# Depthwise convolution taken chunk by chunk, with the next image's normalised input written into freed chunks and an image's gates issued among the next image's taps

## The chip, the cores and the metric

The kernel runs on one NeuronCore of a Trainium2 chip. The metric is the time of one execution on the device, in microseconds; lower is better. Five engines work side by side, each through its own list of instructions, in order: TensorE (PE in the profile, with its weight loads as PEld), VectorE (DVE), ScalarE (ACT), GpSimd (POOL) and SyncE (SP, which here only issues DMAs). An instruction that waits holds up everything behind it in its engine's list.

## What is computed

Two layers over `x` of shape (4, 384, 32, 32): four images, 384 channels, 1024 positions each. All is float32.

```python
x = x + attention(ln_c(x))                 # 8 heads, relative position tables
t = tokens(x); t = t + gelu(ln_t(t) @ w_fc.T) @ w_proj.T      # w_fc, w_proj are Kronecker products
x = image(t)
# layer 1
out = dw(x, w77) + dw(x, w53) + dw(x, w35) + dw(dw(x, w7w), w7h) + dw(dw(x, w5w), w5h) + bias
x = x + out                                # where x inside dw(...) is ln_c(x)
t = tokens(x); u = ln_t(t)
masked = top-2 of softmax(u @ gate_w + gate_b), renormalised      # 4 experts
t = t + sum over e of masked[e] * (gelu(u @ w1[e] + b1[e]) @ w2[e] + b2[e])
```

The five depthwise convolutions are folded into one 7x7 kernel per channel: 49 taps.

## The kernel before

Three phases follow each other. `qkv_phase` writes queries, keys and values to DRAM. `attention_phase` goes through the eight heads and writes `ao_d`; its order is pinned by hand. `rest_phase`, the only one that the change touches, does everything behind the attention. A scheduler lays out its instructions for each engine: what is written earlier in the program comes first, and what is ready may be drawn forward where an engine would otherwise idle by the scheduler's own reckoning. The order on each engine is then fixed.

An image `b` goes through these steps in `rest_phase`. The 384 channels lie as three chunks `k` of 128 partitions, in the tile `xb` (two buffers, so two images at a time).

- `front(b)`: for each half of 512 positions, load `at` (attention output) and the half of `x`, project (L750), add (L753), then the Kronecker feed-forward (L775 to L785).
- `image(xb)`: for each half, statistics over channels (L71 to L79), spread over the partitions (L88, L90), subtract the mean into `xc` (L799, VectorE), multiply by the scale into the padded `img` (L802, GpSimd, all three chunks in one instruction).
- `convolve(b, xb)`: add the bias to `xb` (L813, three instructions), then 49 steps of three taps. A tap is one VectorE instruction, `xb[k] += img[k, shifted] * w7[k]` (L818, 128x1024). The three chunks take turns, so a tap's accumulator was last written three taps earlier. At the end `xb` is stored to `x2_d` (L823).
- `gates(g, b, xb)`: normalise the tokens (L71 to L79, L852), gate scores on TensorE (L537), softmax and top 2 on VectorE (L543 to L571, some forty small instructions that depend on each other).
- `scatter(g)`: after the last image of a group, `slot_positions` computes for each token its slot in a buffer sorted by expert (L617 to L682; L682 writes the weight rows `row`, L663 the slots `pos`), and GpSimd scatters the token rows into `xs_d` by indirect DMA (L862, 16 DMAs per image).

The groups are `((0,), (1,), (2, 3))`. `blocks(g)` runs the experts' feed-forward on blocks of 128 slots: 19 blocks for each of the first two groups, 35 for the third, 73 in all. A block loads its rows (`xg`, L882), transposes them (L888), copies them to `xT` (L889, VectorE), does 36 matmuls `e_ps` (L921) with 12 Gelu instructions (L924) and 12 matmuls `y_ps` (L904), and ends in `yo` (L907, VectorE). The weights of half a block come by an indirect DMA on GpSimd (L894). `combine(g)` gathers two rows per token and adds them to `x2_d`.

The order around the change: image 0 goes through all its steps before any block; `front(1)` runs among the taps of image 0. The steps of images 1 to 3 (`rest_of`) are handed out by `more()`, which `blocks` calls 12 times a block, at a fixed rate over the 38 blocks of the first two groups: 216 steps in 456 calls, one step being three taps. A group's blocks are written only after its own scatter.

Of the kernel before, what the change touches and what calls it, by code (L numbers as in the profile page):

```python
# [10 lines left out]
F32 = mybir.dt.float32  # L11
AF = mybir.ActivationFunctionType
# [5 lines left out]
P = 128  # L18
# [36 lines left out]
def bcast(ap, dim, n):  # L55

    dims = [list(d) for d in ap.ap]
    dims[dim] = [0, n]
    return bass.AP(ap.tensor, ap.offset, dims)


def token_stats(nc, pools, ident, x, eps, rows=None):


    small, psum, tag = pools
    nj = TOK // P
    mv = small.tile([P, nj, 2], F32, tag="s_mv", name="s_mv")
    for j in range(nj):
        ps = psum.tile([P, TOK], F32, tag=tag, name="row_ps")
        for k in range(KC):  # L70
            nc.tensor.transpose(ps[:, k * P : (k + 1) * P], x[:, k, j * P : (j + 1) * P], ident)  # L71
        st = small.tile([P, 6], F32, tag="s_st", name="s_st")
        nc.vector.bn_stats(st, ps[:, :C])  # L73
        nc.vector.bn_aggr(mv[:, j, :], st)
        if rows is not None:
            nc.scalar.copy(rows[j], ps[:, :C])
    rstd = small.tile([P, nj, 1], F32, tag="s_rstd", name="s_rstd")
    nc.scalar.activation(rstd, mv[:, :, 1:2], AF.Sqrt, bias=eps)
    nc.vector.reciprocal(rstd, rstd)  # L79
    return mv[:, :, 0:1], rstd  # L80


def to_partitions(nc, pools, ident, one, values):

    small, psum, tag = pools
    nj = values.shape[1]
    dg = small.tile([P, nj, P], F32, tag="s_dg", name="s_dg")
    nc.vector.tensor_tensor(dg, bcast(ident.unsqueeze(1), 1, nj), bcast(values, 2, P), ALU.mult)  # L88
    ps = psum.tile([P, TOK], F32, tag=tag, name="all_ps")
    nc.tensor.matmul(ps, one, dg.rearrange("p j n -> p (j n)"), start=True, stop=True)  # L90
    return ps
# [593 lines left out]
def rest_phase(tc, cst, x, ao_d, ins, slots, x2_d, out):  # L685
# [9 lines left out]
    with ExitStack() as es:  # L695
# [41 lines left out]
        def front(b, xb):  # L737

            for half in range(2):
                n0 = half * TOK  # L740
                xs = xb[:, :, n0 : n0 + TOK]
                at = ld.tile([P, KC, TOK], F32, tag="at", name="at", bufs=1)
                nc.sync.dma_start(
                    at, ao_d[:, b * N + n0 : b * N + n0 + TOK].rearrange("(k p) n -> p k n", p=P)
                )
# [41 lines left out]
                    )  # L787
                    yield

        def image(xb):  # L790

            rows = IMG // 2
            for half in range(2):
                xs = xb[:, :, half * TOK : (half + 1) * TOK]
                mean, rstd = token_stats(nc, stp, ident, xs, cst["eps6"])
                mps = to_partitions(nc, (small, ps_m, "m"), ident, one, mean)
                sps = to_partitions(nc, (small, ps_m, "m"), ident, one, rstd)
                xc = work.tile([P, KC, TOK], F32, tag="xc", name="xc", bufs=1)
                nc.vector.tensor_tensor(xc, xs, bcast(mps.unsqueeze(1), 1, KC), ALU.subtract)  # L799
                scale_sb = work.tile([P, TOK], F32, tag="scale", name="scale")  # L800
                nc.scalar.copy(scale_sb, sps)
                nc.gpsimd.tensor_tensor(  # L802
                    img[:, :, 3 + half * rows : 3 + (half + 1) * rows, 3 : 3 + IMG],
                    xc.rearrange("p k (y x) -> p k y x", x=IMG),
                    bcast(scale_sb.rearrange("p (y x) -> p y x", x=IMG).unsqueeze(1), 1, KC),
                    ALU.mult,
                )
                yield

        def convolve(b, xb):  # L810

            for k in range(KC):
                nc.vector.tensor_scalar_add(xb[:, k, :], xb[:, k, :], cbias[:, k : k + 1])  # L813
            acc = xb.rearrange("p k (y x) -> p k y x", x=IMG)
            for dy in range(7):
                for dx in range(7):
                    for k in range(KC):
                        nc.vector.scalar_tensor_tensor(  # L818
                            acc[:, k], img[:, k, dy : dy + IMG, dx : dx + IMG], w7[:, k, dy, dx : dx + 1],
                            acc[:, k], ALU.mult, ALU.add,  # L820
                        )
                    yield
            nc.sync.dma_start(x2_d[:, b * N : (b + 1) * N].rearrange("(k p) n -> p k n", p=P), xb)  # L823

        groups = []
# [145 lines left out]
            xbs[b] = xp_.tile([P, KC, N], F32, tag="xb", name="xb")  # L971
            yield from front(b, xbs[b])

        def rest_of(b):

            yield from image(xbs[b])
            ahead = enter(b + 1) if b + 1 < B else iter(())
            for _ in convolve(b, xbs[b]):
                next(ahead, None)
                yield  # L980
            yield from ahead
            yield from gates(owner[b], b, xbs[b])
            if b == owner[b]["images"][-1]:
                yield from scatter(owner[b])
            yield "end"

        def steps_of(images):
            for b in images:
                yield from rest_of(b)

        for _ in enter(0):
            pass
        for _ in rest_of(0):
            pass
        todo = steps_of(range(1, B))
        total = 3 * 62 + 30
        done = [0, 0.0]
        rate = total / (NF * sum(g["nb"] for g in groups[:-1]))
        behind = iter(())
# [113 lines left out]
```

## Time and profile before

| | |
|---|---|
| three timed runs | 3903.89, 3910.33, 3932.67 us (median 3910.33) |
| the profiled execution, its own time | 3887.36 us |
| its span in the profile | 3885.6 us |
| PE busy | 3212.3 us (83%) |
| DVE busy | 2335.8 us (60%) |
| ACT busy | 1250.2 us (32%) |
| POOL busy | 1129.4 us (29%) |
| `rest_phase` (from its first projection to the end) | 1898 to 3886 us |
| taps of image 0 | 2019.05 to 2209.4 us |
| `yo` of block 1, 38, 39 | 2327.33, 3230.36, 3258.34 us |

All durations below come from the profiled execution. Busy time is the union of an engine's instructions; instructions of one engine overlap by a little, so the time from start to start is shorter than the mean duration of one. The number behind `x` is a count.

### The profile page before, as it was taken

The numbers are of one execution on the slowest core, as the hardware profiler recorded it, in microseconds if no ns is written. First come the engines' busy times: TensorE is split into PE (matmuls) and PEld (weight loads), VectorE is DVE, ScalarE is ACT, GpSimd is POOL, SyncE is SP. The second block draws the span as 40 slices with busy tenths as digits, with TensorE's granted clock in tenths as the row PEclk, the third lists the DMA queues.
The fourth block names the chain that finished last, engine by engine and source line by source line (L and its number), as shares of the span: only waits on it lengthen the run. The fifth ranks groups of instructions, "written<-read, shape, count | busy, mean of one in ns | idle before, by whom it ended". The sixth has DMA issues, their size and how long they took to land.

```text
span 3885.6 us, 63554 instructions
## 1 busy us (share of the span) xinstructions
PE 3212.3 (83%) x25493; PEld 2161.8 (56%) x25493; DVE 2335.8 (60%) x3495; ACT 1250.2 (32%) x2502; POOL 1129.4 (29%) x1043
## 2 busy tenths in 40 slices
PE   8977878878787888878665549999998899999993
PEld 4535555555555555545321235574576677777772
DVE  2237777777787877868359958858889921000002
ACT  0124444444444444535111112242232132222220
POOL 3116253535344443526000031131132142111113
PEclk9989999999999998989887569999999899999996
DMA  7344444435363535253200141252143445223304
GB/s 274 127 151 113 132 120 111 139 92 166 71 181 74 181 74 173 72 163 85 76 16 8 37 159 57 106 220 72 66 153 148 152 156 191 79 77 131 130 21 130
DMA packets 195110, 455.06 MB, mean 117 GB/s; under 512 B 67008, under 2 KB 131536, under 8 KB 186880
## 3 DMA queue, kind: packets, MB, share of 16 engines
q1 hardware_dynamic: 145792, 216.99, 18.0%
q0 software_dynamic: 38400, 183.39, 12.8%
q10 hardware_dynamic: 10624, 50.62, 6.1%
q8 instruction: 201, 3.29, 0.4%
q14 instruction: 93, 0.76, 0.1%
HBM read 557.33 MB, written 144.31 MB: 181 GB/s over the span
## 4 chain that ended last, share of the span: by engine, by line
PE 33%; DVE 13%; DMA 3%; issue 2%; POOL 1%; ACT 1%; SPq 0%; POOLq 0%; DVEq 0%; ACTq 0%
PE e_ps L921 13%; PE y_ps L904 12%; DVE xb L818 10%; PE f_ps L775 2%; PE o_ps L778 2%; PE proj_ps L750 1%; DMA yt<-y_d,pos 1%; PE gate_ps L537 1%; PE row_ps L71 1%; DMA w<-in_w,row 1%; PE xT_ps L888 0%; DMA xg<-xs_d 0%; PE ffn_ps L784 0%; DVE xb L813 0%; DVE s_st L73 0%
## 5 line engine op out<-in xcount | busy, mean ns | idle before, releaser
L311 POOL TENSOR_TENSOR bias<-b,s 128x416 f32<-128x416 f32 (+24 forms) x656 | 660.9, 1042 | 829.6 <-DMA qs<-qk_d 502.6
L921 PEld LDWEIGHTS e_ps<-xT,w 128*128 128x128 f32 x5256 | 721.0, 196 | 297.1 <-issue 90.5
L921 PE MATMUL e_ps<-xT,w 128*128 128x128 f32 x5256 | 751.8, 282 | 33.6 <-DVE xT L889 25.1
L904 PE MATMUL y_ps<-w,eh 128*128 128x384 f32 x1752 | 711.4, 492 | 8.6 <-ACT eh L924 8.6
L818 DVE SCALAR_TENSOR_TENSOR xb<-img,w,xb 128x1024 f32<-128x1024 f32 x588 | 712.2, 1274 | 0.0
L924 ACT ACTIVATE eh<-e_ps,w 128x128 f32<-128x128 f32 x876 | 320.0, 367 | 1002.6 <-PE e_ps L921 1001.9
L894 POOL DMA_INDIRECT w<-in_w,row x146 | 214.3, 1468 | 1316.3 <-DVE yo L907 372.9
L354 ACT ACTIVATE arow<-arow,nm 128x1024 f32<-128x1024 f32 x256 | 295.9, 1156 | 297.2 <-DVE nm L344 297.1
L375 ACT COPY aT<-t_ps 128x512 f32<-128x512 f32 x512 | 275.7, 588 | 310.0 <-PE t_ps L374 301.5
L374 PEld LDWEIGHTS t_ps<-ident,arow 128*128 128x128 f32 x2048 | 228.5, 145 | 255.0 <-ACT arow L354 191.9
L202 PE MATMUL sc_ps<-kq,qs 48*32 48x512 f32 x2048 | 291.3, 632 | 88.6 <-DVE nm L344 59.4
L365 DVE TENSOR_REDUCE extra<-arow 128x32 f32<-128x32 f32 (+24 forms) x512 | 356.4, 737 | 0.0
L374 PE MATMUL t_ps<-ident,arow 128*128 128x128 f32 x2048 | 289.8, 286 | 71.1 <-ACT arow L354 56.4
L344 DVE CUSTOM_DVE_ANT_0 arow<-sc_ps,bias 128x1024 f32<-128x1024 f32 x256 | 310.7, 1214 | 36.5 <-POOL bias L311 36.2
L274 DVE STREAM_TRANSPOSE b<-tabk_ps 128x960 f32<-128x960 f32 x128 | 229.3, 1826 | 134.9 <-PE tabk_ps L202 119.8
L202 PE MATMUL tabk_ps<-tab,kq 48*128 48x480 f32 x512 | 261.3, 650 | 37.0 <-DMA kq<-qk_d 29.8
L202 PE MATMUL sc_ps<-k,kq 48*32 48x512 f32 x2048 | 291.3, 632 | 0.0
L904 PEld LDWEIGHTS y_ps<-w,eh 128*128 128x128 f32 x1752 | 272.0, 194 | 22.5 <-ACT eh L924 11.0
L202 PE MATMUL tabq_ps<-tab,kq 48*128 48x480 f32 x512 | 252.9, 639 | 37.0 <-DMA kq<-qk_d 28.3
L907 DVE TENSOR_TENSOR yo<-y_ps,w 128x384 f32<-128x384 f32 x73 | 40.5, 555 | 395.8 <-PE y_ps L904 395.6
L202 PEld LDWEIGHTS av_ps<-aT,vb 128*64 128x64 f32 x4096 | 227.5, 139 | 51.4 <-ACT aT L375 26.0
L202 PE MATMUL av_ps<-aT,vb 128*64 128x128 f32 x4096 | 242.9, 278 | 0.0
(158 smaller groups left out, 3542.2 us busy)
## 6 DMA issues: line engine op xcount, KB each, us to landing
sd<-st SPq DMA_DIRECT2D x128, 480.0 KB, 2.5
s<-sd SPq DMA_DIRECT2D x512, 120.0 KB, 3.0
tvw<-in_tv ACTq DMA_DIRECT2D x120, 192.0 KB, 3.6
xg<-xs_d SPq DMA_DIRECT2D x73, 192.0 KB, 2.4
y_d<-yo SPq DMA_DIRECT2D x73, 192.0 KB, 1.9
qk_d<-qk_sb POOLq DMA_DIRECT2D x48, 256.0 KB, 2.3
kq<-qk_d ACTq DMA_DIRECT2D x16, 768.0 KB, 12.0
v_d<-va POOLq DMA_DIRECT2D x4, 2048.0 KB, 8.0
```

The costliest lines, as they stand in the source:

```text
L202: pin(nc.tensor.matmul(*args, **kw))
L274: nc.vector.transpose(b2.rearrange("p e y x -> p x (e y)")[:, i : i + 2], ps[:, :, : SPAN * IMG])
L311: nc.gpsimd.tensor_tensor(bias[:, y0:y1, :], bass.AP(b2.tensor, b2.offset + (e * IMG + y0) * IMG, [list(b2.ap[0]), [(step * IMG + 1) * IMG ...
L344: nc.vector.tensor_tensor_reduce(s["flat"], ps.rearrange("p h n -> p (h n)"), s["bias"].rearrange("p y x -> p (y x)"), -SCALE, BIG, ALU.ad ...
L354: nc.scalar.activation(s["flat"], s["flat"], AF.Exp, bias=s["nm"], scale=-1.0, accum_out=dn[:, y % YT : y % YT + 1])
L365: pin(nc.vector.tensor_reduce(ex[:, i, :], a[:, p0:p1, :].rearrange("p y x -> p x y"), AX.X, ALU.add))
L374: pin(nc.tensor.transpose(pt[:, j, :], s["flat"][:, k0 : k0 + P], ident))
L375: pin(nc.scalar.copy(aT[:, 4 * g : 4 * g + 4, s["y"] % YB, :], pt))
L818: nc.vector.scalar_tensor_tensor(acc[:, k], img[:, k, dy : dy + IMG, dx : dx + IMG], w7[:, k, dy, dx : dx + 1], acc[:, k], ALU.mult, ALU.add,)
L904: nc.tensor.matmul(py, hs, w[:, o : o + C], start=(ff == 0), stop=(ff == NF - 1))
L921: nc.tensor.matmul(ph, w[:, o : o + P], xT[k][:, c, :], start=(c == 0), stop=(c == KC - 1))
L924: nc.scalar.activation(hs, ph, AF.Gelu, bias=w[:, o : o + 1])
```

## The change

The convolution loop is turned round: the chunk is the outer loop, the 49 taps the inner one, so consecutive taps write the same accumulator. `image` is split. `image_parts(b)` makes `xc` and the scale and adds the bias, now on ScalarE; `image(b, k)` multiplies one chunk into `img` (L812, two instructions of a third of the size), and is called for the next image as soon as the chunk's 49 taps of this image are written and `image_parts` is through. `convolve` now carries a generator `beside(b)`: the gates and scatter of the image before, then `front` and `image_parts` of the next image, one step of it beside two of every three taps. `xc` has two buffers instead of one, and `at` shares them. A step of `todo` is now one tap: 471 steps for the same 456 calls. Image 0's gates and scatter still come before any block.

```diff
-                at = ld.tile([P, KC, TOK], F32, tag="at", name="at", bufs=1)
+                at = work.tile([P, KC, TOK], F32, tag="xc", name="at")
...
+        def image_parts(b):
             for half in range(2):
-                xs = xb[:, :, half * TOK : (half + 1) * TOK]
+                xs = xbs[b][:, :, half * TOK : (half + 1) * TOK]
                 mean, rstd = token_stats(nc, stp, ident, xs, cst["eps6"])
+                yield
...
-                xc = work.tile([P, KC, TOK], F32, tag="xc", name="xc", bufs=1)
+                xc = work.tile([P, KC, TOK], F32, tag="xc", name="xc")
...
+                parts[b].append((xc, scale_sb))
+                yield
+            for k in range(KC):
+                nc.scalar.activation(xbs[b][:, k, :], xbs[b][:, k, :], AF.Identity, bias=cbias[:, k : k + 1])
+            yield
+
+        def image(b, k):
+            rows = IMG // 2
+            for half, (xc, scale_sb) in enumerate(parts[b]):
                 nc.gpsimd.tensor_tensor(
-                    img[:, :, 3 + half * rows : 3 + (half + 1) * rows, 3 : 3 + IMG],
-                    xc.rearrange("p k (y x) -> p k y x", x=IMG),
+                    img[:, k, 3 + half * rows : 3 + (half + 1) * rows, 3 : 3 + IMG],
+                    xc[:, k, :].rearrange("p (y x) -> p y x", x=IMG),
...
-        def convolve(b, xb):
+        def convolve(b, beside):
+            xb = xbs[b]
+            acc = xb.rearrange("p k (y x) -> p k y x", x=IMG)
+            n, free, busy = 0, [], True
             for k in range(KC):
-                nc.vector.tensor_scalar_add(xb[:, k, :], xb[:, k, :], cbias[:, k : k + 1])
-            acc = xb.rearrange("p k (y x) -> p k y x", x=IMG)
-            for dy in range(7):
-                for dx in range(7):
-                    for k in range(KC):
+                for dy in range(7):
+                    for dx in range(7):
                         nc.vector.scalar_tensor_tensor(
                             acc[:, k], img[:, k, dy : dy + IMG, dx : dx + IMG], w7[:, k, dy, dx : dx + 1],
                             acc[:, k], ALU.mult, ALU.add,
                         )
-                    yield
+                        n += 1
+                        if busy and n % 3:
+                            busy = next(beside, None) is not None
+                        if not busy and b + 1 < B:
+                            while free:
+                                image(b + 1, free.pop(0))
+                        yield
+                free.append(k)
+            for _ in beside:
+                pass
+            while free and b + 1 < B:
+                image(b + 1, free.pop(0))
...
+        def dispatch(b):
             yield from gates(owner[b], b, xbs[b])
             if b == owner[b]["images"][-1]:
                 yield from scatter(owner[b])
+
+        def beside(b):
+            if b > 1:
+                yield from marked(dispatch(b - 1))
+            if b + 1 < B:
+                yield from marked(enter(b + 1))
+                yield from marked(image_parts(b + 1))
+
+        def later():
+            for b in range(1, B):
+                yield from convolve(b, beside(b))
+            yield from dispatch(B - 1)
+
+        for steps in (enter(0), image_parts(0)):
+            for _ in steps:
+                pass
+        for k in range(KC):
+            image(0, k)
+        for steps in (convolve(0, beside(0)), dispatch(0)):
+            for _ in steps:
+                pass
+        todo = later()
+        total = 49 * KC * (B - 1) + 30
```

## The prediction

> **What bounds the kernel now.** First the table of stretches of 100 us (columns: length, then busy time and instruction count of PE, PEld, DVE, ACT and POOL, then granted clock, DMA share, GB/s).
>
> ```profile
> 2100.00:2200.00 100.00, 47.71 (x76) 11.97 (x74) 100.00 (x96) 8.90 (x15) 0.00 (x0) 0.58 0.03 8
> 2200.00:2300.00 100.00, 38.38 (x175) 30.94 (x176) 43.74 (x149) 20.25 (x32) 23.16 (x21) 0.58 0.47 180
> ...
> 3000.00:3100.00 100.00, 75.28 (x412) 59.63 (x411) 100.00 (x90) 17.62 (x48) 19.37 (x9) 0.86 0.39 148
> ...
> 3300.00:3400.00 100.00, 100.00 (x616) 79.81 (x615) 6.69 (x12) 27.46 (x75) 12.85 (x13) 1.00 0.23 79
> ```
>
> Three regimes: image 0's taps, VectorE alone (2019 to 2209 us); a hole at 2200 to 2300, neither engine full, where image 0's gates, slots and scatter run; then blocks, where TensorE or VectorE ends last by turns, and from about 3230 us TensorE alone. The chain of waits (start, length, what) says the same of the first two:
>
> ```profile
> 2049.43 38.26 DVE xb L818 x32
> ...
> 2210.76 8.33 PE gate_ps L537 x40
> ...
> 2262.39 17.42 DMA xg<-xs_d
> ```
>
> 32 taps in 38.26 us are 1.196 us from start to start, though one lasts 1.274 on the page: taps on different accumulators overlap. Next, VectorE's own timeline, in image 0's gates, slots and first block, and at the seam between the groups:
>
> ```profile
> 2225.58 0.18 DVE L554 RECIPROCAL g_den<-g_den 128x4 f32<-128x4 f32 x1
> 2225.79 0.18 DVE L555 TENSOR_TENSOR g_pr<-g_pr,g_den 128x16 f32<-128x16 f32 x1
> 2226.00 0.17 DVE L563 TENSOR_TENSOR g_more<-g_pr 128x16 f32<-128x16 f32 x1
> 2226.09 0.16 DVE L562 TENSOR_TENSOR g_more<-g_pr 128x4 f32<-128x4 f32 x1
> 2226.17 0.16 DVE L563 TENSOR_TENSOR g_more<-g_pr 128x12 f32<-128x12 f32 x1
> ...
> 2237.36 0.17 DVE L663 CAST pos<-p_fpos 128x16 uint32<-128x16 f32 x1
> ...
> 2274.41 0.56 DVE L889 COPY xT<-xT_ps 128x384 f32<-128x384 f32 x1 [36.74 <-PE xT_ps L888]
> ...
> 2290.46 3.51 DVE L88 TENSOR_TENSOR s_dg<-ident,s_mv 128x512 f32<-128x512 f32 x1
> ```
>
> ```profile
> 3230.36 0.56 DVE L907 TENSOR_TENSOR yo<-y_ps,w 128x384 f32<-128x384 f32 x1 [15.23 <-PE y_ps L904]
> ...
> 3258.34 0.55 DVE L907 TENSOR_TENSOR yo<-y_ps,w 128x384 f32<-128x384 f32 x1
> ```
>
> The first three depend each on the one before: 0.21 us from start to start at 0.18 long. The next two are free: 0.08 to 0.09 at 0.16. A dependent instruction waits out its predecessor and some 0.035 more. Block 1 starts 37 us after L663 (2237.36 to 2274.41), through 16 scatter DMAs of 1.275 us and the load of `xg`. `yo` of block 38 stands at 3230.36, of block 39 at 3258.34. Last, the instructions around `img` (minimum/median/maximum ns):
>
> ```profile
> L802 POOL TENSOR_TENSOR img<-xc,scale x8: 3421/3585/3933, 2007.9 to 2913.0; 128x1536 f32<-128x1536 f32 x8
> ...
> L813 DVE TENSOR_SCALAR xb<-xb,cbias x12: 740/753/3934, 2014.2 to 2913.3; 128x1024 f32<-128x1024 f32 x12
> ```
>
> L813 takes 3.93 instead of 0.75 us where it meets L802; so does the L88 above, 3.51 instead of 0.69.
>
> **The change, part by part.**
>
> *A tap now waits for the tap before.* 1.275 + 0.035 = 1.31 us instead of 1.196 wherever two taps of one chunk are neighbours. The Trainium skill, page "VectorE: DVE Perf Modes", section "The DRAIN you can't avoid", says that a semaphore between VectorE instructions costs nothing extra; by it the tap would stay at 1.196 us and the sum below would be some 10 us less before the blocks. The small rows above speak for a price.
>
> *Image 0's taps carry other work.* In the scheduled order of the changed kernel, VectorE has between image 0's first tap and the first statistic of its gates 147 taps of image 0, already 29 taps of image 1 (the two alternate at the end), and the two `xc` of image 1 with their statistics. 94 free taps x 1.196 = 112.4; 82 held x 1.31 = 107.4; the rest (12 adds at 0.66, 2 L799 at 1.7, 32 statistics, 6 L88) 27.0: 246.8 us. The same sum for before is 147 x 1.196 + 15.0 = 190.8, and the trace has 190.35.
>
> *Start.* L813 goes to ScalarE: three instructions of about 1.16 us (L354, the same shape), beside GpSimd's first products, which the first tap also waits for; uncovered, 1.2 us once. Before, the second `xc` ended at 2013.64, L813 met L802, and the first tap came at 2019.05. Now one product of a third (3.585 / 3 = 1.2) lies between: first tap about 2015.2.
>
> *Products beside taps.* The 24 small products cost GpSimd the same 28.7 us. Ten (four of image 0, six of image 1) now lie beside taps; before, none did. By the L813 and L88 rows a tap could be held by a whole product: 10 x 1.2 = 12 us; if not, 0. I take 6: a tap is neither of those instructions, but L88 also reads two SBUF tensors. The Trainium skill, "SBUF — State Buffer", section "Who interferes with whom", speaks against the change here: two SBUF inputs contend with a GpSimd instruction that reads SBUF, and the later one blocks wholly. By it 12 us stand here, not 6.
>
> *`at` shares the ring of `xc`*, so `at` of image 1 waits for GpSimd's half-0 products, about 2012 us; 4.7 us to land and 2.6 of matmuls bring L753 by 2020, and VectorE meets it after six taps, at 2023. Nothing; up to 4 us if late.
>
> So image 0's taps end at 2015.2 + 246.8 + 6 = 2268, not 2209.
>
> *Gates and slots of image 0.* Before: 28 us from the last tap to L663, 18.5 of it busy. Now 27 taps of image 1 stand among these small dependent instructions: 18.1 + 33, plus about 4 of the 9.5 us of waiting that the taps don't cover: 55. L663 at 2323, 86 later. Block 1's first L889 follows 37 us later as before (17 taps fill 21 of these): 2360. From there to `yo` 1 VectorE has 30 taps (38 us) and 7 us else; before it took 53. `yo` 1 about 2405 instead of 2327: **+78**. All of this is on the path: no block can start before image 0's scatter.
>
> *The blocks of groups 0 and 1.* The early taps come back here. For each of the 37 intervals between `yo` 1 and `yo` 38 I add up both engines' instructions from their lists (TensorE 0.43 us per 512 columns and pass, from 18 projections in 7.74 us; an empty block 16.0) and take the larger. Before: 834; trace: 903. The 69 missing lie mostly where an image changes (intervals 2, 10, 13, 22, 23, 32), in chains that neither sum shows. After: 799, since 103 taps instead of 15 are done by `yo` 1 and a block with no other work holds 13 taps (17 us, near TensorE's 16) where it held 18 (22.5). Fewer such chains remain on the path, so I put 6% on top instead of 8: 850. **-53.**
>
> *Seam to group 2.* Before, L663 of group 2 stood at 3139.74, 75 us ahead of `yo` 37, and 32 scatter DMAs ran beneath three blocks. Now 441 single taps use up 441 of the 471 steps, image 3's gates come last, and L663 stands just before `yo` 37 (the matmul in front of it at 36.2 blocks). From there: 32 x 1.275 = 41, then 16 us as in group 0 (last scatter, `xg`, transpose, `xT`): 57; a block, 18; less 23 until `yo` 38: 52 us from `yo` 38 to 39, against 28. **+24.** The weight DMAs of group 2's first block queue behind these scatters on GpSimd and land in the same time. Its blocks then run as before.
>
> Gates of images 1 and 2 and the scatter of group 1 stay covered: five blocks still follow the latter. GpSimd's products for images 2 and 3 stand between weight loads, as L802 did.
>
> Sum: +78 - 53 + 24 = **+49 us**: 3887.4 + 49 = 3936 for a profiled execution. The profiled execution of before is 0.6% under the median of its runs (3910.33); on that scale 3960.
>
> **The rivals.**
>
> *The blocks give it all back.* The 69 us vanish wholly, because the chains at an image change (statistics, L802, L813, first tap) are what the change takes off the path: 799 instead of 850. For it: 3000 to 3100 us has TensorE at 75%, and VectorE has slack afterwards. Against: gates still come in one piece, and `front` still waits on ScalarE and VectorE in turn. It gives -2 on the sum, about 3908: not slower. It decides where the 37 intervals take under about 837 us. If group 2's scatter is hidden too, about 3883. For faster by over 1% the blocks must also start 20 us sooner than I sum.
>
> *Taps and products cost their upper bounds.* 12 us of products, taps at 1.4 us (98 held ones before the blocks, +9), the blocks 8% above their sum (865), and VectorE-bound stretches longer by as much again: 3990 to 4015.
>
> *It does not do what it says.* The early taps never free VectorE, because in intervals 4, 5 and 17 to 19 the list holds none and VectorE waits for the next image. That is in the 799 already; worth 0 to +15.
>
> **How the numbers follow.** About 1% (39 us) is what a measurement of this kernel can tell from no change. The forecast, slower by 10 to 90 us, gets 0.62, a quarter of it under 39; the give-back 0.22, with 0.04 more for a scatter and start better than summed; the upper bounds 0.12. Slower by over 1%: 0.46 + 0.12, about 0.59. Faster by over 1%: 0.08, since both ends of the blocks' sum are loose. The rest, 0.33, within. The range reaches from the give-back with half the scatter hidden (3895) to the upper bounds (4015).
>
> **What would show it.** Start to start of neighbouring taps on one chunk (1.31, not 1.196); L663 of image 0 near 2323; `yo` 1 near 2405; 37 intervals in about 850; `yo` 39 some 50 us after `yo` 38, with TensorE idle between; taps longer beside L812. Wrong if the intervals take under 837, or if `yo` 1 comes before 2380.

## The result, and the profile after

| | before | after |
|---|---|---|
| four timed runs each, on one chip: median (lowest to highest) | 3915.52 us (3903.89 to 3932.67) | 3955.17 us (3950.06 to 3967.41) |
| ratio to before, with its 95% interval | | 1.0102 (1.0056 to 1.0148) |
| the profiled execution, its own time | 3887.36 us | 3956.91 us |

The changed kernel is slower by 1.0%. Its profiled execution lies on the median of its runs, where that of before lay 0.7% under its own: so the two profiled executions differ by 69.5 us, the medians by 39.7. What follows takes the profiles apart; of the ratios, those in the table of experiments decide.

From one profiled execution to another the first tap of image 0 comes between 1999 and 2039 us, with next to nothing changed ahead of it, so from here on time is counted from that tap (2019.00 us in the profile of before, 2015.96 in that of after).

| us | before | after | difference |
|---|---|---|---|
| first tap to image 0's last tap | 190.4 | 270.3 | +79.9 |
| from there to image 0's slots (L663) | 28.0 | 53.1 | +25.1 |
| to the first `xT` | 37.0 | 40.6 | +3.6 |
| to `yo` 1 | 52.9 | 48.2 | -4.7 |
| `yo` 1 to `yo` 37 | 887.2 | 814.2 | -73.0 |
| `yo` 37 to `yo` 39 | 43.8 | 84.8 | +41.0 |
| `yo` 39 to the end | 627.3 | 627.8 | +0.5 |
| sum | 1866.6 | 1939.0 | +72.4 |

First the stretches of 100 us that were shown of before (length, busy us and count of PE, PEld, DVE, ACT and POOL, granted clock, DMA share, GB/s), with 3200 to 3300 in place of the next, and then two stretches cut to measure:

```profile
2100.00:2200.00 100.00, 53.20 (x94) 15.55 (x93) 76.74 (x81) 14.19 (x21) 2.93 (x2) 0.54 0.00 0
2200.00:2300.00 100.00, 14.49 (x65) 13.31 (x65) 93.88 (x95) 4.48 (x9) 75.06 (x4) 0.50 0.09 31
...
3000.00:3100.00 100.00, 96.49 (x579) 78.50 (x579) 91.70 (x146) 37.03 (x83) 23.18 (x10) 0.95 0.45 172
...
3200.00:3300.00 100.00, 59.45 (x354) 45.20 (x353) 22.49 (x120) 26.77 (x53) 41.28 (x43) 0.81 0.45 171
...
2046.70:2068.70 22.00, 19.13 (x48) 4.01 (x48) 16.18 (x15) 7.84 (x13) 0.00 (x0) 1.00 0.00 1
2102.70:2139.60 36.90, 32.72 (x48) 5.97 (x48) 16.17 (x15) 9.30 (x14) 0.00 (x0) 0.54 0.00 0
```

Between 2100 and 2200, where VectorE was full before, it is busy 77 us of 100: image 0's taps have got holes. The hole at 2200 to 2300 is full of taps now: up to 2286 the last of image 0's and, in turn with them, 29 of image 1's. TensorE's 75% at 3000 to 3100 has become 96%, and a new hole stands at 3200 to 3300. The last two lines are the two halves of image 1's Kronecker feed-forward (L769 to L781): the same 48 matmuls take 22.0 us at a granted clock of 1.00 and 36.9 us at 0.54. VectorE is busy some 16 us in either, with 13 taps.

VectorE's timeline (start, length, engine, line; in brackets the idle time ahead and what ended it) at the places that were shown of before:

```profile
2068.71 0.69 DVE L781 COPY o<-o_ps 128x512 f32<-128x512 f32 x1 [5.83 <-PE o_ps L778]
...
2139.64 0.69 DVE L781 COPY o<-o_ps 128x512 f32<-128x512 f32 x1 [20.77 <-PE o_ps L778]
...
2169.24 117.10 DVE L828 SCALAR_TENSOR_TENSOR xb<-img,w,xb 128x1024 f32<-128x1024 f32 x97
...
2339.40 0.16 DVE L663 CAST pos<-p_fpos 128x16 uint32<-128x16 f32 x1
...
2379.98 0.56 DVE L910 COPY xT<-xT_ps 128x384 f32<-128x384 f32 x1 [19.95 <-PE xT_ps L909]
...
2428.16 0.56 DVE L928 TENSOR_TENSOR yo<-y_ps,w 128x384 f32<-128x384 f32 x1 [1.41 <-PE y_ps L925]
...
3235.01 0.17 DVE L663 CAST pos<-p_fpos 128x32 uint32<-128x32 f32 x1
...
3242.34 0.56 DVE L928 TENSOR_TENSOR yo<-y_ps,w 128x384 f32<-128x384 f32 x1 [6.99 <-PE y_ps L925]
3284.05 0.56 DVE L928 TENSOR_TENSOR yo<-y_ps,w 128x384 f32<-128x384 f32 x1 [41.15 <-PE y_ps L925]
...
3327.16 0.56 DVE L928 TENSOR_TENSOR yo<-y_ps,w 128x384 f32<-128x384 f32 x1 [3.28 <-PE y_ps L925]
```

Three things are to be seen. VectorE waits 26.6 us for image 1's feed-forward, which 31 or 32 taps covered before. It ends image 0 in a row of 97 taps, 29 of them image 1's. And the slots of group 2 are there only 7.3 us ahead of `yo` 37 (before: 74.8), so its first block ends 84.8 us behind `yo` 37. Last, the instructions around `img` (minimum/median/maximum ns):

```profile
L812 POOL TENSOR_TENSOR img<-xc,scale x24: 1261/1270/70404, 2010.5 to 2908.7; 128x512 f32<-128x512 f32 x24
...
L828 DVE SCALAR_TENSOR_TENSOR xb<-img,w,xb x588: 1244/1276/2300, 2016.0 to 3137.3; 128x1024 f32<-128x1024 f32 x196
```

Where they meet, both can suffer. A product that takes 1.27 us took 70.4, beneath the row of 97 taps, which kept 1.207 us from start to start. And by VectorE's timeline eight taps took 2.07 to 2.30 us instead of 1.28, each of them beside a product; the taps' median hides that (1276 against 1275 ns). Besides, the page's groups show VectorE waiting for L812 5.2 us in all.

### The profile page after: what moved, and what is told of

Read it like the earlier page. It is cut to its first block, busy times and chain, and to the rows that moved or that the text cites. A ratio compares the mean times of both kernels' runs of the same rounds, so it can differ in the third digit from the quotient of the medians.

```text
span 3955.0 us, 63598 instructions
## 1 busy us (share of the span) xinstructions
PE 3200.0 (81%) x25493; PEld 2150.7 (54%) x25493; DVE 2326.3 (59%) x3483; ACT 1258.0 (32%) x2511; POOL 1202.7 (30%) x1059
## 4 chain that ended last, share of the span: by engine, by line
PE 35%; DVE 11%; issue 2%; DMA 2%; POOL 1%; ACT 1%; another core or an unknown queue 1%; SPq 0%; POOLq 0%; DVEq 0%; ACTq 0%
PE e_ps L942 13%; PE y_ps L925 12%; DVE xb L828 8%; PE o_ps L778 3%; PE f_ps L775 2%; PE proj_ps L750 1%; DMA xg<-xs_d 1%; DMA yt<-y_d,pos 1%; PE gate_ps L537 1%; PE ffn_ps L784 1%; POOL yt L970 1%; PE xT_ps L909 1%; PE row_ps L71 0%; DVE s_st L73 0%
## 5 line engine op out<-in xcount | busy, mean ns | idle before, releaser
L942 PEld LDWEIGHTS e_ps<-xT,w 128*128 128x128 f32 x5256 | 716.1, 193 | 255.7 <-issue 66.1
L942 PE MATMUL e_ps<-xT,w 128*128 128x128 f32 x5256 | 740.1, 278 | 8.8 <-DMA w<-in_w,row 3.3
L828 DVE SCALAR_TENSOR_TENSOR xb<-img,w,xb 128x1024 f32<-128x1024 f32 x588 | 730.2, 1288 | 7.2 <-POOL img L812 5.2
L915 POOL DMA_INDIRECT w<-in_w,row x146 | 203.4, 1393 | 1112.5 <-DVE yo L928 400.0
L344 DVE CUSTOM_DVE_ANT_0 arow<-sc_ps,bias 128x1024 f32<-128x1024 f32 x256 | 310.6, 1213 | 39.7 <-POOL bias L311 39.5
L925 PEld LDWEIGHTS y_ps<-w,eh 128*128 128x128 f32 x1752 | 268.2, 193 | 40.6 <-ACT eh L945 21.9
L202 PE MATMUL tabk_ps<-tab,kq 48*128 48x480 f32 x512 | 259.3, 647 | 38.2 <-DMA kq<-qk_d 29.4
```

Source lines behind the costliest of these rows:

```text
L202: pin(nc.tensor.matmul(*args, **kw))
L344: nc.vector.tensor_tensor_reduce(s["flat"], ps.rearrange("p h n -> p (h n)"), s["bias"].rearrange("p y x -> p (y x)"), -SCALE, BIG, ALU.ad ...
L828: nc.vector.scalar_tensor_tensor(acc[:, k], img[:, k, dy : dy + IMG, dx : dx + IMG], w7[:, k, dy, dx : dx + 1], acc[:, k], ALU.mult, ALU.add,)
L925: nc.tensor.matmul(py, hs, w[:, o : o + C], start=(ff == 0), stop=(ff == NF - 1))
L942: nc.tensor.matmul(ph, w[:, o : o + P], xT[k][:, c, :], start=(c == 0), stop=(c == KC - 1))
```

## The experiments

All ratios are to the kernel before on the same chip (its median there was 3891, 3916, 3920, 3893 and 3888 us in the five groups e1 to e4, e5 to e8, e9 and e10, e11, e12), with 95% intervals. The four columns of stretches are from one profiled execution each, counted as above; the last is the sum of the two before it. These executions do not all stand alike to the runs of their kernel: that of before lies 28 us under its median, those of e1 and e3 13 and 14 us under, those of e7 and e12 23 and 19 us over, the others within 9 us.

| | ratio | to `yo` 1 | `yo` 1 to 37 | 37 to 39 | 1 to 39 |
|---|---|---|---|---|---|
| before (first comparison) | 1 | 308.3 | 887.2 | 43.8 | 931.0 |
| after (first comparison) | 1.0102 (1.0056 to 1.0148) | 412.2 | 814.2 | 84.8 | 899.0 |
| e1 turned loop alone | 1.0087 (1.0070 to 1.0104) | 324.4 | 904.0 | 46.0 | 950.0 |
| e2 image 1's taps held back | 1.0026 (1.0007 to 1.0045) | 363.7 | 822.2 | 80.8 | 903.0 |
| e3 steps 12% faster | 1.0139 (1.0122 to 1.0156) | 410.0 | 837.9 | 45.1 | 883.0 |
| e4 image 1's front spread | 1.0055 (1.0038 to 1.0072) | 375.1 | 807.0 | 80.7 | 887.7 |
| e5 after, again | 1.0121 (1.0088 to 1.0155) | 415.3 | 828.6 | 88.3 | 916.9 |
| e6 faster for image 3 only | 1.0119 (1.0081 to 1.0158) | 408.2 | 864.8 | 45.0 | 909.8 |
| e7 e2 + e4 + e6 | 0.9916 (0.9889 to 0.9944) | 336.9 | 857.2 | 45.0 | 902.2 |
| e8 gates in steps of their own | 1.0116 (1.0079 to 1.0152) | 408.7 | 819.1 | 92.0 | 911.1 |
| e9 e7 + scatter paced | 0.9876 (0.9852 to 0.9899) | 336.9 | 855.8 | 42.1 | 897.9 |
| e10 norm in one piece | 1.0118 (1.0079 to 1.0156) | 408.4 | 833.8 | 79.4 | 913.2 |
| e11 before, finer steps | 0.9953 (0.9931 to 0.9974) | 305.2 | 877.5 | 46.8 | 924.3 |
| e12 e2 + e4, steady, paced | 0.9919 (0.9897 to 0.9941) | 358.8 | 830.3 | 44.2 | 874.5 |

**e1: the loop turned, alone.** In the kernel before:

```diff
-            for dy in range(7):
-                for dx in range(7):
-                    for k in range(KC):
+            n = 0
+            for k in range(KC):
+                for dy in range(7):
+                    for dx in range(7):
                         nc.vector.scalar_tensor_tensor(...)
-                    yield
+                        n += 1
+                        if n % KC == 0:
+                            yield
```

> The kernel before with the convolution's loop turned round and nothing else: chunk outside, taps inside, three taps a step. If a tap waits out the tap before it at 1.31 us (the prediction's step), image 0's 147 taps take 17 us more, `yo` 1 comes near 2344 instead of 2327.33, and the whole is 17 to 45 us slower than before, the more the more blocks VectorE ends. If neighbouring taps on one chunk cost the same 1.2 us as free ones (what 97 taps in 117.10 us in the changed kernel say), the taps of image 0 end within 2 us of before, start to start stays at 1.20, and the whole is within 0.3% of before.

It is slower by 0.9%, and the second reading, which I held, falls. From the first tap `yo` 1 comes 16.1 us later, the blocks take 16.8 us more. VectorE's timeline in image 0:

```profile
2131.10 39.56 DVE L819 SCALAR_TENSOR_TENSOR xb<-img,w,xb 128x1024 f32<-128x1024 f32 x33
...
2180.32 39.59 DVE L819 SCALAR_TENSOR_TENSOR xb<-img,w,xb 128x1024 f32<-128x1024 f32 x30
```

33 taps take as long as the last 30. With the last tap's own 1.28 us taken off, the first row runs at 1.196 us from start to start, the second at 1.321. The built program's list tells them apart once each tap is read with its chunk: in the first row the scheduler has put taps of two chunks in turn; the last 30 are all of the third chunk, each on the accumulator that the tap before it wrote. So the dependence does cost 0.125 us a tap, the prediction's price, but only where neighbours are of one chunk, and of image 0's 147 taps in this kernel only 29 are. The start-to-start times of all neighbouring taps agree: in image 0, 29 lie at 1.32 us here and none in the changed kernel; in the blocks it is 75 here and 55 there. In the changed kernel's image 0 none is: there the scheduler took image 1's taps as the lone chunk's partners. That also tells why 97 taps in 117.10 us (1.207 each) showed no price: it was not a row of dependent taps. The dependent ones make 3.6 us. A wait of 19.49 us at L781 is more, as in the changed kernel: in the first half only 13 taps stand there, at a granted clock of 0.52, though the front is given out at the pace of before. Image 0's last tap comes 24.3 us later in all, of which 8 are made up by `yo` 1.

**e2: image 1's taps behind image 0's slots.** In the changed kernel, `mark` being the last instruction of `slot_positions`:

```diff
-                        nc.vector.scalar_tensor_tensor(
+                        tap = nc.vector.scalar_tensor_tensor(
...
+                        if b == 1 and dy + dx == 0:
+                            tc.add_manual_dep(tap.ins, groups[0]["mark"].ins.name, NoSync, ...)
```

> The changed kernel, with the first tap of each chunk of image 1 held behind image 0's slots (a dependence in the list of VectorE, no wait). Theory: image 1's taps ahead of image 0's last ones and among its gates are what sets the start back; without them image 0's last tap comes near 2251 instead of 2286, the slots near 2283 instead of 2339, `yo` 1 near 2365 instead of 2428. In the whole that is worth some 15 us (3940), since the taps not done early come back where VectorE ends the blocks of group 0. First rival: they come back wholly, the time stays at 3955 within 8. Second rival: the blocks have room for them, and the whole gains 45 us or more (3910).

```profile
2161.20 87.68 DVE L828 SCALAR_TENSOR_TENSOR xb<-img,w,xb 128x1024 f32<-128x1024 f32 x68
...
2279.42 0.17 DVE L663 CAST pos<-p_fpos 128x16 uint32<-128x16 f32 x1
...
2371.58 0.56 DVE L934 TENSOR_TENSOR yo<-y_ps,w 128x384 f32<-128x384 f32 x1 [1.41 <-PE y_ps L931]
```

On VectorE's timeline the row of 97 taps has become 68, 29.4 us shorter, though 28 of image 0's taps are dependent neighbours now. Image 0's slots come 271.5 us behind the first tap instead of 323.4, `yo` 1 48.5 us sooner. The blocks give back only 8.0 us (nothing against e5, on another chip), though by the built lists 54 fewer taps, some 65 us of VectorE, are done by `yo` 1. The ratio falls from 1.010 or 1.012 to 1.003: the taps drawn ahead were nearly pure loss.

**e3: steps handed out 12% faster.**

```diff
-        total = 49 * KC * (B - 1) + 30
+        total = 1.12 * (49 * KC * (B - 1) + 30)
```

> The changed kernel, with the steps handed out 12% faster, so that image 3's gates and the scatter of group 2 are through some three blocks sooner. Theory: the seam costs 41 us because 32 scatters begin 7 us before the end of block 37 and nothing is left to run beside them; with blocks beside them `yo` 37 to `yo` 39 falls from 84.8 us to 45 to 55 (before: 43.8), and the whole from 3955 to about 3922. Rival, the prediction's smaller seam of 24: 3932. Rival: the last block of group 1 stalls by itself (ScalarE's last three Gelus wait 4 to 12 us each, not traced to the scatter), and stalls again: 3940 to 3950. Rival: the faster handing out slows the blocks of groups 0 and 1 by as much as the seam gains: 3955.

The seam went as expected (45.1 us), the time did not: three of the four runs took 3940 to 3948 us (the profiled one 3928), no less than the changed kernel against its own before. Against e4 and e2 on the same chip, which have the changed kernel's seam, `yo` 1 to 37 is 30.9 and 15.7 us longer. By the ratio the last rival holds; the profiled run, the fastest of the four, shows only part of it, since its `yo` 1 to 39 is shorter than the changed kernel's (883.0 against 899.0).

**e4: image 1's front spread.**

```diff
-                        if busy and n % 3:
+                        if busy and (n % 3 if b else n % 3 == 0):
```

> The changed kernel, with image 1's front spread over image 0's taps as before the change (one step beside every third tap instead of beside two of three). Theory: VectorE's waits at L781 (5.83 and 20.77 us) come from 12 Gelu rounds covered by 13 taps; spread out they fall under 5 us in sum, image 0's last tap comes 20 us or more sooner (2266), `yo` 1 at about 2400 instead of 2428, the whole near 3935. Rival: the wait moves to the statistics of image 1's norm or to its first tap, since image 1's front ends later; `yo` 1 within 5 us of 2428 and the whole at 3955. The seam should stay at about 41 us above before; if ScalarE's late Gelus in block 38 are an accident of one execution, they are not there, and `yo` 37 to `yo` 39 is 65 to 75 us instead of 84.8.

```profile
2068.26 0.69 DVE L781 COPY o<-o_ps 128x512 f32<-128x512 f32 x1 [5.83 <-PE o_ps L778]
...
2163.61 0.70 DVE L781 COPY o<-o_ps 128x512 f32<-128x512 f32 x1
```

The wait of 20.77 us is gone, that of 5.83 is not: 33 taps stand in the second half now, but still 13 in the first. Image 0's last tap comes 39.2 us sooner after the first: 20.8 of the wait, the rest from fewer taps of image 1 among its last ones. The time falls by half of what the change had cost. The seam stays at 80.7 us though the late Gelus of block 38 are absent; block 38 then takes 14.4 us and block 39 66.2. So they are not what the seam costs.

**e5 to e8.** e5 is the changed kernel once more. e6 and e8 change one thing in it, e7 joins e2, e4 and e6. The edits of e6 and e8:

```diff
-                done[1] += rate
+                done[1] += rate * (1.4 if done[0] >= 49 * KC * (B - 2) else 1)
```

```diff
-            if b > 1:
-                yield from marked(dispatch(b - 1))
...
                 yield from convolve(b, beside(b))
-            yield from dispatch(B - 1)
+                yield from dispatch(b)
...
-        total = 49 * KC * (B - 1) + 30
+        total = 49 * KC * (B - 1) + 44
```

> The changed kernel once more, unchanged, on the chip of the other three, so that they can be set against it. From the first tap of image 0: `yo` 1 at 412 us, then 814 to `yo` 37, 80 to 85 to `yo` 39, 628 to the end. Rival: the stall of block 38 (ScalarE's late Gelus) was an accident of the first execution; then `yo` 37 to `yo` 39 takes under 70.

The late Gelus and the seam came again.

> The changed kernel, handing out steps 1.4 times as fast from image 3's convolution on, and not before. Theory: its taps are drawn ahead by the scheduler and end by block 32 in any case, while VectorE sits idle until the gates in block 36; so three blocks come between the scatter and the seam, and `yo` 37 to `yo` 39 falls from 84.8 to about 45 us, with `yo` 1 to `yo` 37 at 814 within 8. Whole: 36 us or so less than the changed kernel, level with before (ratio 0.998 to 1.003). Rival (what the 12% faster handing out did): the blocks lose 20 us or more of it again. Rival: it is the last block that stalls, not the scatter that comes late; `yo` 37 to `yo` 39 stays over 65.

The seam fell to 45.0 us and `yo` 1 to `yo` 37 rose by 36.2 us against e5: the same cost in another place. Block 34, which now runs beside the 32 scatter DMAs, takes 49.16 us. ScalarE's timeline in it:

```profile
3186.33 0.37 ACT L945 ACTIVATE eh<-e_ps,w 128x128 f32<-128x128 f32 x1 [3.19 <-PE e_ps L942]
3191.31 0.37 ACT L945 ACTIVATE eh<-e_ps,w 128x128 f32<-128x128 f32 x1 [4.62 <-remote]
3201.21 0.37 ACT L945 ACTIVATE eh<-e_ps,w 128x128 f32<-128x128 f32 x1 [9.53 <-remote]
3220.18 0.37 ACT L945 ACTIVATE eh<-e_ps,w 128x128 f32<-128x128 f32 x1 [18.61 <-remote]
3222.35 0.62 ACT L945 ACTIVATE eh<-e_ps,w 128x128 f32<-128x128 f32 x2 [1.80 <-remote]
```

A Gelu comes every 1.3 us beside the first scatters (from 3175.28); then each waits longer than the one before, the last two about twice as long, until the last scatter is out (3216). By TensorE's timeline the matmuls that the first four read had started 5, 8, 17 and 33 us earlier. In the kernel before, 32 scatters ran beneath three blocks without this, at most 6 of them in a row without a weight load.

> The three mends together: image 1's taps behind image 0's slots, image 1's front spread over image 0's taps, and the faster handing out from image 3's convolution on. Theory (each loss is by itself, and the gain in the blocks needs none of what causes them): from the first tap, `yo` 1 at about 338 us (363.7 with the first mend alone, less the 20.8 us of waiting at L781), 815 to `yo` 37, 45 to `yo` 39, 628 after: 1826, against 1866.5 before and 1939 in the changed kernel, so a ratio to before near 0.98. Rival: the blocks need the early taps; without them `yo` 1 to `yo` 37 is 850 or more and the ratio 1.00.

A ratio of 0.992, the first version faster than before. `yo` 1 stands at 336.9 us; e2's 363.7 less the 20.8 us of e4's wait are 342.9 (the expectation's 338 was a slip), so the two losses at the start are separate. The blocks took 857 us, not 815, with the slow block 34 (49.1 us) as in e6. The expected ratio was worked out a per cent too low. By its stretches alone this profiled execution, the slowest of its six runs, is no faster than that of before; that it is faster rests on the ratio.

> The changed kernel, with the gates and the scatter of images 1 to 3 issued in steps of their own behind the image's taps, as before the change, and not beside the next image's taps. Theory: the gain of 73 us in the blocks comes from an image's gates lying among the next image's taps; `yo` 1 stays at 412 us from the first tap and `yo` 1 to `yo` 37 goes from 814 to 860 or more. Rival: it comes from the next image's norm and products lying ready when its first tap is due; then it stays at 815 to 830. Whole: 45 us more than the changed kernel, or as much.

The gain stays, as the rival said: 819.1 us, and 911.1 to `yo` 39 against 916.9 in e5 on the same chip. Issuing gates among the next image's taps is worth nothing here.

**e9: the scatter paced; e10: the norm in one piece.** e9 is e7 with three steps for two scatter DMAs; e10 is the changed kernel with `image_parts(b + 1)` and the products behind the last tap for images 2 and 3.

```diff
                     done.append(ins_)
-                yield
+                for _ in range(3):
+                    yield
```

```diff
-                        if not busy and b + 1 < B:
+                        if not busy and b == 0:
...
             for _ in beside:
                 pass
+            if 0 < b < B - 1:
+                for _ in image_parts(b + 1):
+                    pass
...
                 yield from marked(enter(b + 1))
-                yield from marked(image_parts(b + 1))
+                if b == 0:
+                    yield from marked(image_parts(b + 1))
```

> The three mends together, and the scatter handed out in three steps for every two DMAs instead of one, so that weight loads come between the scatter DMAs in GpSimd's list (the longest run without one is 14, where it was 32). Theory: what the faster handing out gained at the seam it lost in block 34 (49.2 us), since 32 scatters in a row take GpSimd for 41 us and blocks slow down beside them, which they didn't in the kernel before, where at most 6 stood in a row. In shorter runs no block beside the scatter takes over 32 us, `yo` 19 to `yo` 37 falls from 369 to about 345, and the ratio to before from 0.992 to about 0.985. Rival: the number of scatters counts and not their order; the blocks lose the same 30 us spread over more of them, and the ratio stays at 0.992.

0.988, the best of these ratios, though on a chip other than e7's. Block 34 takes 34.4 us instead of 49.1, with Gelus still waiting up to 8.9 us in the run of 14. But block 33, ahead of the scatter, takes 52.0 us instead of 31.7: in it TensorE waits 16.50 us at L71 for the taps of image 3, whose gates follow there in one piece. The two blocks together took longer than in e7. `yo` 1 to `yo` 37 did not fall: the part up to `yo` 19 took 458.5 us (488.4 in e7), the part behind it 397.3 instead of the expected 345.

> The changed kernel, with the norm (statistics, xc, bias) and the products of images 2 and 3 issued in one piece behind the last tap of the image before, not beside its taps and into freed chunks. Theory: the gain of 73 to 90 us between `yo` 1 and `yo` 37 comes from the next image's norm and products lying ready when its first tap is due; then it goes from 814 to 828 back to 860 or more. Rival: it comes from more even handing out alone (14 taps in a block where VectorE had 19 and TensorE waited for it); then it stays within 10 us of 814 to 828. `yo` 1 stays at 412 us from the first tap in either case.

833.8 against 828.6 in e5 (on another chip), the same ratio: by its range the rival holds. The norm lying ready is not what the blocks gained by.

**e11: the kernel before with finer steps.** One tap a step, `front` beside every third tap as before, a matching rate:

```diff
                             acc[:, k], ALU.mult, ALU.add,
                         )
-                    yield
+                        yield
...
-            for _ in convolve(b, xbs[b]):
-                next(ahead, None)
+            for i, _ in enumerate(convolve(b, xbs[b])):
+                if i % KC == KC - 1:
+                    next(ahead, None)
...
-        total = 3 * 62 + 30
+        total = 560
```

and a second `yield` behind each pair of scatter DMAs.

> The kernel before, loop and gates as they were, with one tap to a step instead of three (one step of the next image's front still goes beside every third tap), two steps for every two scatter DMAs, and a rate to match (560 steps). Theory: what the change gained between `yo` 1 and `yo` 37 is neither the gates beside taps nor the norm lying ready, but taps handed out more evenly: before, 18 to 20 taps stand in a block of image 3 and VectorE takes 22.5 us for them where TensorE takes 16; with 14 or 15 such a block takes 17 to 18. `yo` 19 to `yo` 37 falls from 387 to 350 or so, `yo` 1 stays at 308 from the first tap, and the ratio to before is 0.99. Rival: the taps taken out of image 3's blocks come back as more of them, and the sum stays within 8 us of 387 (ratio 1.00).

0.995: a small gain, but not the one looked for. Image 3's blocks did fall from 22.5 to 18.9 us, with 15 taps instead of 18. But there were more of them, and blocks 22 and 23, where the image changes, took 75.3 us instead of 61.6: `yo` 19 to `yo` 37 is 386.2 against 387.3, so the rival holds for that stretch. The 12 scatters that stand in a row here delayed no Gelu.

**e12: a steady rate, shorter runs of scatters.** e2 and e4 with the pacing of e9 and

```diff
-        total = 49 * KC * (B - 1) + 30
+        total = 1.08 * (49 * KC * (B - 1) + 78)
```

> The first two mends (image 1's taps behind image 0's slots, its front spread), with three steps for every two scatter DMAs and one rate from the start that ends seven blocks before the seam; in GpSimd's list at most 8 scatter DMAs of group 2 stand in a row. Theory: ScalarE's late Gelus come with a long run of scatter DMAs; with runs of 8 or less none waits over 3 us beside them, no block beside the scatter takes over 30 us, and `yo` 1 to `yo` 39 takes 870 us where the other version (e9) took 898; from the first tap 337 + 870 + 628 = 1835, and a ratio to before of 0.98. Rival: the late Gelus come in runs of 8 too. Rival: handing out faster from the start costs the blocks of group 0 as much; `yo` 1 to `yo` 39 stays at 895 or more and the ratio at 0.988.

The three blocks beside the scatters, cut at their `yo`s:

```profile
3106.84:3122.62 15.78, 15.78 (x98) 12.58 (x97) 0.56 (x1) 4.41 (x12) 11.92 (x13) 1.00 0.61 229
3122.62:3139.95 17.33, 16.35 (x101) 12.78 (x100) 1.12 (x3) 4.41 (x12) 11.91 (x13) 1.00 1.00 385
3139.95:3155.81 15.86, 15.04 (x89) 11.43 (x88) 1.11 (x2) 3.67 (x10) 10.22 (x11) 1.00 0.70 270
```

GpSimd issues 37 DMAs in them, most of them the scatter's, and TensorE has next to no hole: 15.8 to 17.3 us a block. No Gelu waited over 3 us. `yo` 1 to `yo` 39 takes 874.5 us, as expected. `yo` 1 came at 358.8 instead of 337: the first half of image 1's feed-forward ran at a granted clock of 0.55, and VectorE waited 19.43 us at L781 where it had waited 5.83 in e7. So this version is not settled as better or worse than e9; both beat both kernels.

## Why the prediction was right, and where it was not

It said slower by 10 to 90 us, 3960 us likeliest; the median is 3955, and all runs lie in its range. By the profiled executions its sum was +49 against +69.5, and the medians are closer to it because the two profiled executions stand differently to theirs. That the median comes within 5 us of 3960 is luck: by the traces the start was summed 23 us too short, the blocks 6 us too short and the seam 9 us too long. Its steps, one by one:

*A tap waits for the tap before.* The price was right (1.31 predicted, 1.321 in e1), the number wrong: "82 held" counted neighbours on one tile, and the tile holds three chunks. Image 0 has no such neighbours in the changed kernel, so 9.4 us of the sum were not there. The Trainium skill, "VectorE: DVE Perf Modes", "The DRAIN you can't avoid", says that a semaphore between VectorE instructions costs nothing extra; a tap that needs its neighbour's result starts 0.125 us later in e1, and the measurement decides.

*Image 0's list.* The missing term is a wait. The list was summed by its instructions, and before, no wait stood there. In the changed kernel 13 taps instead of 31 or 32 cover each of the two chains of twelve Gelu rounds: 26.6 us at L781. In the second half that comes from the pace of the front, which the change doubles: with the old pace e4 has 33 taps there, and the 20.77 us are gone. In the first half it comes with the turned loop: e1 and e4, which have the old pace, hold 13 taps there too. In spite of the 9.4 us that were not there, image 0's last tap came 18 us later than the predicted 2268.

*Start, products, `at`.* The first tap was predicted at 2015.2 and came at 2015.96; since that tap moves by 40 us between executions, what counts is that it came 1.75 us behind the second `xc`, where before it came 5.4 us behind. `at` cost nothing: VectorE met L753 behind six taps without a wait. For the products beside taps 6 us were taken: four taps before `yo` 1 ran about 1.0 us longer beside one, 4 us in all. The waiting for L812 is besides, 1.74 us at the first tap and 3.48 in the blocks. The rule of the skill that was weighed there ("SBUF — State Buffer", "Who interferes with whom") is right in that the two contend; but the 12 us worked out by it did not come, a tap lost 1.0 us and not a product's 1.27, and beneath the row of 97 taps it was GpSimd that lost.

*Gates, slots, first block.* 55 us predicted, 53.1 measured; `xT` after 40.6 instead of 37 and `yo` 1 after 48.2 instead of 45. With the list this makes `yo` 1 at 2428 instead of 2405: +100.8 against the predicted +78.

*The blocks.* -53 was predicted from `yo` 1 to `yo` 38; the trace has -47.1 there, -73.0 to `yo` 37. But e6 shows that blocks and seam are one sum: 36 to 43 us go from one to the other with the place of group 2's scatter. Taken together, `yo` 1 to `yo` 39, the prediction has -29 and the trace -32. Its reason does not hold in that size: "the early taps come back here", but 54 of them are worth 8 us in e2.

*The seam.* +24 was predicted for `yo` 38 to `yo` 39 (52 us against 28); they lie 43.1 us apart, +15.1. But block 38 had taken 41.7 us instead of 15.8, with the late Gelus, which the prediction did not have, so that from `yo` 37 on it is +41.0. From L663 to `yo` 39 the prediction summed 75 us, and the trace has 92.2. The 32 scatters took 41 us as summed, and the first `xT` came 20 us behind them (16 summed). The step that failed is the block, which ends 29 us behind its `xT` instead of 18. Its DMAs had been put at nothing (they "land in the same time"). A stretch of the table, then TensorE's timeline:

```profile
3284.00:3304.00 20.00, 1.81 (x7) 1.00 (x6) 3.57 (x7) 0.00 (x0) 5.84 (x6) 0.50 0.98 388
```

```profile
3306.27 0.88 PE L909 MATMUL xT_ps<-ident,xg 128*128 128x128 f32 x3 [6.60 <-DMA xg<-xs_d]
3306.94 3.84 PE L942 MATMUL e_ps<-xT,w 128*128 128x128 f32 x18
```

The DMA engines are at 98%, and TensorE begins the block's matmuls (L942) 8.8 us behind its `xT` (3298.16): a third group of transposes stands ahead of them and waits 6.60 us for its rows. The granted clock is 0.50 up to 3308. Whether the weights too came late is not shown, since the trace has no landing for them.

*What stays open.* Where all of the 32 us between `yo` 1 and `yo` 39 come from. Gates beside taps (e8), the norm ahead (e10) and finer steps in the old kernel (e11: 6.7 us) each account for little or nothing, and 54 of the 88 early taps for 8 us. The stretch from `yo` 1 to `yo` 39, before and after, says where to look:

```profile
2327.33:3258.34 931.01, 863.60 (x4426) 591.70 (x4426) 680.32 (x951) 265.96 (x596) 230.97 (x152) 0.95 0.36 132
2428.16:3327.16 899.00, 827.91 (x4399) 576.96 (x4400) 563.47 (x854) 265.27 (x592) 225.94 (x160) 0.96 0.37 137
```

TensorE stands idle 67.4 us of it before and 71.1 after: the stretch is shorter by TensorE's busy time, not by its waits. It holds 27 matmuls fewer, mostly the first of image 2's feed-forward, which in the changed kernel stand ahead of `yo` 1 and take some 14 us there. The other 21 us of busy time are not traced to a cause. The products by chunk and the bias on ScalarE were not tried alone. The rival "the blocks give it all back" fell by its own condition: `yo` 1 to `yo` 38 took 855.9 us, not under 837. Nor was the second rival met: neither taps nor products cost their upper bounds. The third is right in what it names, VectorE without taps in some blocks, but that was in the sum.

## What to carry to other kernels

Read a list of instructions with the part of the tile that each writes: whether neighbours depend on one another, and what the scheduler draws in between them, is not seen by the tile's name. Work that is put "beside" an engine's long row has to be spread so that each of its chains is covered, at the slow clock too; and work drawn ahead of a result that another engine waits for is paid in full there, even if it is free later. Where a serial piece (here 32 scatter DMAs) is moved into covered time, look at what it does to the cover: e6 gained 43 us in one place and lost 36 in the other. And when a stretch gets shorter, look whether it still holds the same work.

## What the hardware showed that was not expected

- A VectorE tap that reads the accumulator which its neighbour has just written starts 1.321 us behind it, one that doesn't 1.196 us (e1).
- Beneath the row of 97 taps, free of each other, a GpSimd product of 1.27 us took 70.4 us, while the taps kept 1.21 us; it was the same in e3, e5, e6, e8 and e10. In e2, where the taps at that place are dependent neighbours, the two products took 2.24 us each, and the two taps beside them 2.2 us from start to start.
- The issue of a scatter DMA on GpSimd took about 2.0 us at every second one while taps ran back to back (six of image 0's sixteen, 1.80 to 2.04 us), and 0.97 us without them. In e2 to e10 eight of the first nine took 1.79 to 2.09 us.
- ScalarE's Gelus beside a long run of scatter DMAs waited 4.6, 9.5, 18.6 us in turn (e6), with all that the program makes them wait for done by the profile. It was seen in the changed kernel, e5, e6, e7, e9 and e10, with runs of 14 to 32; not in e11 and e12 with runs of 12 and 8, but not in e3 either, with 26, on another chip, where Gelus ran beside the scatters for 24 us. e2, e4 and e8, with 32, decide little: there the last Gelu of block 38 came before 21 us of scatters were out, and in the others the first late one came 11 to 24 us behind the first scatter. Whether the run's length or the chip decides it, and what the Gelus wait for, is open.
- The same 48 matmuls and 12 Gelus took 22.0 us at a granted clock of 1.00 and 36.9 us at 0.54.
